# Spreading 1/rms rows by PE transposes, small column loads on the SP queue, and shared-expert parts dealt over 28 experts

## The chip, the cores and the metric

The kernel runs on one core of one Trainium2 chip. Its time is the device time of one launch in microseconds (us), the median of several runs. The profile is one execution recorded by the hardware profiler; its stages are given as us from the start of its span.

## The reference

Four sequences of 512 tokens with 512 features pass through a cross-attention layer and a mixture-of-experts layer. Cut to what matters:

```python
x = x + xattn(layernorm(x), ctx)        # ctx: 4 x 1601 x 512, the first 257 rows are image rows
x = x + ffn(layernorm(x))

# xattn: 16 heads of 32
q = rms_norm(x @ q_w.T + q_b, norm_q_w)             # norm over all 512 features
k = rms_norm(ctx_txt @ k_w.T + k_b, norm_k_w); v = ctx_txt @ v_w.T + v_b
k_img, v_img = ...                                  # the same with the image weights
out = (attention(q, k, v) + attention(q, k_img, v_img)) @ o_w.T + o_b

# ffn: 32 experts of width 256, 4 chosen per token, at most 80 tokens per expert
Y = (silu(Xp @ W_gate) * (Xp @ W_up)) @ W_down      # Xp: the tokens of each expert
out = scatter_add(Y * weight)
shared = (silu(x @ sg.T) * (x @ su.T)) @ sd.T       # width 512, for all tokens
return out + shared
```

Everything is computed in float32; only the shifts of the softmax are split into bfloat16 parts.

## The kernel before, in words

The order of all instructions is written out by hand: each engine executes its instructions in the order in which the program issues them, and buffers are rings of named tiles, so an instruction waits for its operands, and for its output's buffer to be read out.

**Start.** SP and ACT each issue a part of the first loads. ACT issues the four pieces of the key weight `first_wk`, two of the four tiles of x, and then, by `column` (L153 to L156), eight small columns of biases and norm weights and `o_b` (L197). A bias column is read with a stride, 512 elements of 4 bytes (`"(c p) -> p c"`). SP issues the first context block, the other two x tiles, four pieces of `q_w` and then whole blocks and weights. On TensorE (PE) the projections of the first context block run with the input chunk k outermost, over four PSUM banks: k = 0, 1, 2, then k = 3 (L636 to L649). Between them stand the tasks of the four x tiles: `norm` (ACT, L273) makes the layer-normed `xl`, `turn` (L279, L280) transposes it on PE, four 128x128 blocks a tile, and ACT copies it to `xlT`. Before the change two tiles are turned behind k = 2 and two behind k = 3. After them the projections of q from `xlT` begin.

**Keys and queries, per sequence b.** `feature_chunk` (L228) projects a block of keys or queries, four chunks of 128 features. ACT squares each (L235), DVE applies bias and norm weight (L236), GpSimd (POOL) sums the squares (L238). `norms` (L247) sums over features by matmuls with a column of ones, and POOL makes the column `r` of 1/rms, one value per token. `normed` (L253 to L261) needs that column as a row spread over all 128 partitions: for each 128 tokens PE multiplies the column, broadcast to [128, 128] as the stationary operand, by the identity, and DVE multiplies the chunk by the result in PSUM (L261). There are five calls per sequence: q, three text blocks (512, 512, 320 tokens) and the image block (257). Between them DVE takes the maxima of the first scores (L310).

**Attention.** Scores, exponentials (L374), sums and weighted values, with the maxima (L336) of the next chunk alongside.

**Experts.** The shared expert is cut into units. For the token blocks n = 0 to 2 they run ahead of the routed experts. The twelve units of the last block, n = 3 (eight gate/up projections, four down projections), form the list `between`. The loop over the 32 routed experts does for expert e: `gate_up(e)`, the gather of the tokens of expert e + 7 (POOL), `turn(e + 2)`, `down(e - 1)`, the weight loads of expert e + 4 (SP), and then those units of `between` that are due (L1104). In `down`, ACT scales the result to `y` (L1030, four buffers) and POOL issues an indirect DMA that adds its 80 rows into `out` (L1031). Each of these scatters waits until the previous one has landed, since all write `out`. The last down unit of the shared expert copies its part to `ys`, and POOL issues one DMA that adds 1024 KB into `out` (L977); it stands in the same chain of writers.

Of the kernel before, what the change touches and what calls it, by code (L numbers as in the profile page):

```python
# [18 lines left out]
P = 128  # L19
# [10 lines left out]
E, I, TOPK, NG, TKG = 32, 256, 4, 8, 3  # L30
# [28 lines left out]
@with_exitstack  # L59
def xattn_moe_kernel(ctx: ExitStack, tc: tile.TileContext, a: dict, out: bass.AP):  # L60
    nc = tc.nc

    dram = ctx.enter_context(tc.tile_pool(name="dram", bufs=1, space=DRAM))
    x1_d = dram.tile([T, D], F32, name="x1_d")

    xw_d = dram.tile([T, D + E], F32, name="xw_d")
    xnT_d = dram.tile([P, NC, T], F32, name="xnT_d")
    den_d = dram.tile([B * NC, 2 * NG4, L], F32, name="den_d")
    rec_d = dram.tile([B * NC, 2 * NG4, L], F32, name="rec_d")

    const = ctx.enter_context(tc.tile_pool(name="const", bufs=1))
    ident = const.tile([P, P], F32, name="ident")
    make_identity(nc, ident)
    mhalf = const.tile([P, 8], F32, name="mhalf")
    nc.gpsimd.memset(mhalf, -0.5)
    logits = const.tile([P, NT, E], F32, name="logits")

    with tc.manual_schedule():
        body(tc, a, ident, mhalf, logits, x1_d, xw_d, xnT_d, den_d, rec_d, out)
# [30 lines left out]
def body(ctx, tc, a, ident, mhalf, logits, x1_d, xw_d, xnT_d, den_d, rec_d, out):  # L110

    nc = tc.nc
# [12 lines left out]
    def psum(dt=F32):  # L125

        shape = [P, 512] if dt is F32 else [P, NQ, P]
        banks.append(banks.pop(0))
        return ring.tile(shape, dt, name="ps", tag=f"bank{banks[-1]}")
# [17 lines left out]
    def rowt(name):  # L147
        return row.tile([P, D], F32, name=name, tag="row")
# [3 lines left out]

    def column(name, src=None):  # L153
        t = w.tile([P, NC], F32, name=name, tag=name)
        nc.scalar.dma_start(t, a[name] if src is None else src)
        return t  # L156

    def bias_column(name):
        return column(name, a[name].rearrange("(c p) -> p c", p=P))
# [6 lines left out]
    def load_x(b, qt, queue=nc.sync):  # L166
        xt = rowt("xt")
        queue.dma_start(xt, a["x"][b, qt * P:(qt + 1) * P, :])
        return xt
# [13 lines left out]
    for k in range(NC):  # L183
        nc.scalar.dma_start(first_wk[:, k, :], a["k_w"][:, k, :])
        nc.sync.dma_start(first_block[:, k, :], a["ctxT"][0, k * P:(k + 1) * P, s0:s0 + n])
        if k in (1, 2):
            first_x += [load_x(0, len(first_x), nc.scalar), load_x(0, len(first_x) + 1)]
    for k in range(NC):
        nc.sync.dma_start(wq[:, k, :], a["q_w"][:, k, :])
    k_b, nk_w = bias_column("k_b"), column("norm_k_w")  # L190
    q_b, nq_w = bias_column("q_b"), column("norm_q_w")
    second_block = load_block(0, 1)
    wv = weight("v_w")
    ki_b, nki_w = bias_column("k_img_b"), column("norm_k_img_w")
    v_b, vi_b = bias_column("v_b"), bias_column("v_img_b")
    o_b = w.tile([P, D], F32, name="o_b")
    nc.scalar.dma_start(o_b, a["o_b"].partition_broadcast(P))  # L197
    rw = w.tile([P, NC, E], F32, name="rw")
    ones = w.tile([P, P], F32, name="ones")
    nc.gpsimd.memset(ones, 1.0)  # L200
# [26 lines left out]
    def feature_chunk(dst, xT, n, wt, bias, weights, c, ps, sq, k, at=0):  # L227


        to = slice(at, at + n)  # L230
        nc.tensor.matmul(ps[:, :n], lhsT=wt[:, k, c * P:(c + 1) * P], rhs=xT[:, k, to], start=k == 0, stop=k == NC - 1)  # L231
        if k < NC - 1:
            return
        s = rowt("sq")[:, :n] if c else sq[:, to]
        nc.scalar.activation(s, ps[:, :n], AF.Square, bias=bias[:, c:c + 1])  # L235
        nc.vector.tensor_scalar(dst[:, c, to], ps[:, :n], bias[:, c:c + 1], weights[:, c:c + 1], ALU.add, ALU.mult)  # L236
        if c:
            nc.gpsimd.tensor_tensor(sq[:, to], sq[:, to], s, ALU.add)  # L238
        elif n % P:
            nc.gpsimd.memset(sq[:, n:n + P - n % P], 1.0)  # L240
# [12 lines left out]
    def normed(dst, r, n):  # L253

        ps = psum()
        for s in range(-(-n // P)):
            m = min(P, n - s * P)
            nc.tensor.matmul(
                ps[:, s * P:s * P + m], lhsT=r[:, s:s + 1].to_broadcast([P, P]), rhs=ident[:, :m], start=True, stop=True
            )  # L260
        nc.vector.tensor_tensor(dst, dst, ps[:, :n].unsqueeze(1).to_broadcast([P, NC, n]), ALU.mult)  # L261

    def turned_x(xlT, qt, xt):
# [218 lines left out]
    def queries(b, xs, n):  # L482

        qT = kv.tile([P, NC, L], F32, name="qT", bufs=2)
        xlT = kv.tile([P, NC, L], F32, name="xlT", tag="xlT")
        sq = held("sq_q")
        turn = [turned_x(xlT, qt, lambda qt=qt: xs[qt]) for qt in range(NQ)]

        def part(c, at):
            ps = psum()  # L490
            for k in range(NC):
                feature_chunk(qT, xlT, n, wq, q_b, nq_w, c, ps, sq, k, at)

        return qT, sq, turn, [partial(part, c, at) for c in range(NC) for at in range(0, L, n)]
# [135 lines left out]
    qT, sq_q, turn, work = queries(0, first_x, L)  # L630
# [4 lines left out]
    for k in range(NC):  # L635
        if k == NC - 1:  # L636
            first_sq = rowt("sq_k")
            nc.vector.tensor_scalar(nq_w, nq_w, SM_SCALE, None, ALU.mult)
        for c, ps in enumerate(first_banks):
            feature_chunk(first_kT[:, :, :n], first_block, n, first_wk, k_b, nk_w, c, ps, first_sq if k == NC - 1 else None, k)  # L640
        if k == 0:
            turn[0][1]()
            turn[1][1]()
        if k == 2:
            for qt in (0, 1):
                turn[qt][2]()
                turn[qt + 2][1]()
    for qt in (2, 3):
        turn[qt][2]()  # L649
    ident_b = w.tile([P, P], BF16, name="ident_b")  # L650
    nc.vector.tensor_copy(ident_b, ident)

# [21 lines left out]
    for n in range(2):  # L674
        t = w.tile([P, NQ, P], BF16, name=f"parts{n}", tag=f"parts{n}")
# [6 lines left out]
    for b in range(B):  # L682
# [51 lines left out]
        def take_normed(x):  # L734
            k0 = 0 if x == "q" else BLOCKS[x][0]
            normed(qT if x == "q" else kT[:, :, k0:k0 + size(x)], rs[x], size(x))
# [60 lines left out]
        for c in range(NC):  # L797
# [7 lines left out]
            fill, done = [], 0  # L805
# [22 lines left out]
            for t in range(NKT):  # L828
# [8 lines left out]
                if t == 1:  # L837
                    if more:
# [3 lines left out]
                        done = 1  # L842
# [30 lines left out]
                if prepares:  # L873
                    if t == 0:
                        xs = []
                        qT_next, sq_next, turn, work = queries(b + 1, xs, P)
# [28 lines left out]
    def expert_weights(e):  # L905
        ws = []
        for name, shape in (("W_gate", [P, NC, I]), ("W_up", [P, NC, I]), ("W_down", [P, NI, D])):
            t = wgp.tile(shape, F32, name=name, tag=name)
            nc.sync.dma_start(t, a[name][e])
            ws.append(t)  # L910
        return ws
# [143 lines left out]
    weights, gather, turn, gate_up, down = expert_parts()  # L1055
# [36 lines left out]
    n_between, done = len(between), 0  # L1092
    for e in range(E + 1):
        if e < E:
            gate_up(e)
            if e + AHEAD < E:
                gather(e + AHEAD)
        if e + 2 < E:
            turn(e + 2)
        if e:  # L1100
            down(e - 1)
            if e + WEIGHTS - 1 < E:
                weights[e + WEIGHTS - 1] = expert_weights(e + WEIGHTS - 1)
        while done < n_between and done * (E - 15) < n_between * (e + 1):  # L1104
            between.pop(0)()
            done += 1

# [36 lines left out]
```

## Time and profile before

| | us |
|---|---|
| median of three runs | 1740.51 (1738.91 to 1740.76) |
| the profiled execution, its own time | 1738.34 |
| its span, first to last instruction | 1736.6 |
| PE busy | 1688.6 (97%) |
| DVE busy | 982.7 (57%) |
| POOL busy | 865.2 (50%) |
| ACT busy | 649.4 (37%) |
| first routed expert's activation (L1020) | starts at 1491.5 |
| last scatter (L1031) | starts at 1729.06 |

A busy PE is not PE at its peak, since the ends of matmuls are modelled. The page's rows give engine, line, output and inputs, shapes, count, busy us and mean ns of one; a row of the timeline begins with the start and the length in us, and ends, in brackets, with the engine's idle time before it and what ended that.

### The profile page before, as it was taken

To read this page: it belongs to the slowest core of one execution; us is meant where nothing else is said; L and a number is where in the kernel's file an instruction comes from. 1 tells how busy PE (TensorE), PEld (TensorE's weight loads), DVE (VectorE), ACT (ScalarE), POOL (GpSimd) and SP (SyncE) were. 2 spreads that over 40 slices of the span, in tenths; PEclk is the share of its full clock that TensorE was granted. 3 is DMA by queue.
4 is the path that set the end of the run, shared out by engine and by line. 5 is a ranking of instruction groups with operands and counts; after the bars stand their busy time and mean duration, and the time that the engine had idled before them with its cause. 6 is when DMAs were issued, how large, how long until landed. Compare 5 with 4: busy or idle time off the path is not lost. (4 is left out here: it accounts for less than half of the span.)

```text
span 1736.6 us, 29529 instructions
## 1 busy us (share of the span) xinstructions
PE 1688.6 (97%) x11825; PEld 890.4 (51%) x11825; DVE 982.7 (57%) x2016; ACT 649.4 (37%) x1378; POOL 865.2 (50%) x615
## 2 busy tenths in 40 slices
PE   8999999999999999999999999999999999999993
PEld 3564444456544444564444445644442454666772
DVE  4765554857555557967666579666557665111110
ACT  2135456611355565115555641255547110111110
POOL 3237977332668853327679523296792210323232
PEclk9999999999999999999999999999999999999997
DMA  7000000312000004020001040300012563587882
GB/s 229 1 2 1 27 27 2 114 63 69 30 2 26 27 15 150 21 79 13 27 2 27 14 162 8 110 8 14 2 38 87 172 218 95 183 258 245 281 282 34
DMA packets 68344, 137.34 MB, mean 79 GB/s; under 512 B 16112, under 2 KB 28528, under 8 KB 66160
## 3 DMA queue, kind: packets, MB, share of 16 engines
q1 hardware_dynamic: 58336, 121.73, 20.6%
q0 software_dynamic: 5648, 11.87, 3.4%
q10 hardware_dynamic: 4224, 1.87, 0.4%
q8 instruction: 93, 1.52, 0.4%
q14 instruction: 43, 0.35, 0.1%
HBM read 112.63 MB, written 22.81 MB: 78 GB/s over the span
## 5 line engine op out<-in xcount | busy, mean ns | idle before, releaser
L374 ACT ACTIVATE pT<-ps 128x512 f32<-128x512 f32 (+1 forms) x832 | 429.7, 603 | 342.2 <-PE ps L373 331.8
L336 DVE TENSOR_REDUCE mx<-ps 128x1 f32<-128x512 f32 (+1 forms) x576 | 330.8, 616 | 264.7 <-PE ps L322 264.7
L389 POOL TENSOR_TENSOR acc<-acc,pT 128x1024 f32<-128x1024 f32 x192 | 445.7, 2360 | 3.0 <-ACT pT L374 2.6
L381 PE MATMUL po<-pT,v 128*32 128x512 f32 (+2 forms) x1792 | 222.0, 603 | 0.0
L292 PEld LDWEIGHTS ps<-v_w,cT 128*128 128x128 f32 (+1 forms) x1408 | 168.9, 186 | 102.2 <-DVE mx L336 56.1
L373 PE MATMUL ps<-qT,kT 32*128 32x512 f32 (+1 forms) x1664 | 213.7, 587 | 0.0
L322 PE MATMUL ps<-kT,qT 32*128 32x512 f32 (+1 forms) x1536 | 206.1, 549 | 0.0
L292 PE MATMUL ps<-v_w,cT 128*128 128x128 f32 (+1 forms) x1408 | 197.7, 284 | 0.0
L231 PE MATMUL ps<-cT,wk 128*128 128x512 f32 (+1 forms) x384 | 155.2, 549 | 6.1 <-DMA wk<-in_k_w 6.1
L310 DVE TENSOR_REDUCE mx<-ps 128x1 f32<-128x512 f32 (+2 forms) x256 | 128.2, 563 | 5.6 <-PE ps L307 5.6
L1031 POOL DMA_INDIRECT out<-y,tok x32 | 45.4, 1418 | 160.3 <-ACT y L1030 91.3
L1021 DVE TENSOR_TENSOR ehT<-ehT,ps 128x160 f32<-128x160 f32 x32 | 10.3, 322 | 177.2 <-ACT ehT L1020 162.8
L231 PEld LDWEIGHTS ps<-cT,wk 128*128 128x128 f32 x384 | 70.3, 192 | 75.9 <-issue 54.9
L370 PEld LDWEIGHTS <-pick 32*128 32x128 bf16 (+1 forms) x832 | 21.6, 91 | 165.8 <-issue 164.1
L300 ACT COPY v<-ps 128x128 f32<-128x128 f32 (+1 forms) x208 | 59.7, 287 | 118.4 <-PE ps L292 117.9
L238 POOL TENSOR_TENSOR sq_k<-sq_k,sq 128x512 f32<-128x512 f32 (+2 forms) x48 | 49.7, 1035 | 104.9 <-ACT sq L235 104.6
L396 POOL TENSOR_TENSOR acc<-pT 128x1024 f32<-128x1024 f32 x24 | 56.1, 2362 | 87.0 <-ACT pT L374 54.4
L389 POOL TENSOR_TENSOR pT<-pT 65x1024 f32<-65x1024 f32 x24 | 56.0, 2354 | 86.6 <-PE po L381 77.8
L389 DVE TENSOR_TENSOR acc<-acc,pT 128x1024 f32<-128x1024 f32 (+1 forms) x72 | 97.7, 1404 | 2.1 <-ACT pT L374 2.1
L322 PEld LDWEIGHTS ps<-kT,qT 32*128 32x128 f32 x1536 | 82.0, 183 | 30.8 <-issue 10.1
L381 PEld LDWEIGHTS po<-pT,v 128*32 128x32 f32 (+2 forms) x1792 | 34.7, 107 | 118.6 <-issue 109.3
L370 PE MATMUL ps<-mT,pick 32*128 32x512 bf16 (+1 forms) x832 | 82.5, 385 | 2.5 <-ACT mT L361 2.5
(209 smaller groups left out, 2207.3 us busy)
## 6 DMA issues: line engine op xcount, KB each, us to landing
W_gate<-in_W_gate SPq DMA_DIRECT2D x32, 512.0 KB
W_up<-in_W_up SPq DMA_DIRECT2D x32, 512.0 KB
W_down<-in_W_down SPq DMA_DIRECT2D x32, 512.0 KB
rb<-rec_d SPq DMA_DIRECT2D x64, 128.0 KB
xt<-in_x SPq DMA_DIRECT2D x30, 256.0 KB
cT<-in_ctxT SPq DMA_DIRECT2D x7, 1024.0 KB
wki<-in_k_img_w SPq DMA_DIRECT2D x4, 1024.0 KB
wo<-in_o_w SPq DMA_DIRECT2D x4, 1024.0 KB
```

What stands on the lines that cost most here:

```text
L231: nc.tensor.matmul(ps[:, :n], lhsT=wt[:, k, c * P:(c + 1) * P], rhs=xT[:, k, to], start=k == 0, stop=k == NC - 1)
L292: nc.tensor.matmul(ps[lo:hi, :], lhsT=cTs[bl][:, k, at:at + hi - lo], rhs=ws[bl == NB - 1][:, k, c * P:(c + 1) * P], start=k == 0, stop=k ...
L300: nc.scalar.copy(v[:n, t, :], ps[:n])
L310: nc.vector.tensor_reduce(mx[:, qt, g, bl:bl + 1], ps[:, :n], AX.X, ALU.max, negate=True)
L322: nc.tensor.matmul(ps[:, j * n:(j + 1) * n], lhsT=qT[r:r + HD, c, q * P:(q + 1) * P], rhs=kT[r:r + HD, c, k0:k0 + n], start=True, stop=True,)
L336: nc.vector.tensor_reduce(mx[:, qt, g, i:i + 1], ps[:, :m], AX.X, ALU.max, negate=True)
L370: nc.tensor.matmul(ps[:n], lhsT=pick[r:r + HD, kind(t), :n], rhs=mT[r:r + HD, :], start=True, stop=False)
L373: nc.tensor.matmul(ps[:n], lhsT=kT[r:r + HD, c, t * P:t * P + n], rhs=qT[r:r + HD, c, :], start=False, stop=True)
L374: nc.scalar.activation(pT[:n, g, :], ps[:n], AF.Exp)
L381: nc.tensor.matmul(po[r:r + HD, :], lhsT=v[rows, t, r:r + HD], rhs=pT[rows, g, :], start=start, stop=stop)
L389: (nc.vector if idle else nc.gpsimd).tensor_tensor(to[rows, h, :], to[rows, h, :], pT[rows, h, :], ALU.add)
L396: (nc.vector if idle else nc.gpsimd).tensor_tensor(acc[:, h, :], pTs[0][:, h, :], pTs[1][:, h, :], ALU.add)
```

## The change

It has three parts. In `normed` the matmul with the identity becomes a PE transpose of the broadcast column; for a last part of m tokens only m rows are read. In the start, the small columns and `o_b` go to the SP queue, those of k ahead of `q_w`; and the turns stand one step earlier: two tiles behind k = 1 and two behind k = 2. In the loop over the experts the twelve units are dealt over 28 experts in place of 17: the last one comes behind expert 25 instead of 15.

```diff
     def column(name, src=None):
         t = w.tile([P, NC], F32, name=name, tag=name)
-        nc.scalar.dma_start(t, a[name] if src is None else src)
+        nc.sync.dma_start(t, a[name] if src is None else src)
...
+    k_b, nk_w = bias_column("k_b"), column("norm_k_w")
     for k in range(NC):
         nc.sync.dma_start(wq[:, k, :], a["q_w"][:, k, :])
-    k_b, nk_w = bias_column("k_b"), column("norm_k_w")
     q_b, nq_w = bias_column("q_b"), column("norm_q_w")
...
-    nc.scalar.dma_start(o_b, a["o_b"].partition_broadcast(P))
+    nc.sync.dma_start(o_b, a["o_b"].partition_broadcast(P))
...
             m = min(P, n - s * P)
-            nc.tensor.matmul(
-                ps[:, s * P:s * P + m], lhsT=r[:, s:s + 1].to_broadcast([P, P]), rhs=ident[:, :m], start=True, stop=True
-            )
+            nc.tensor.transpose(ps[:, s * P:s * P + m], r[:m, s:s + 1].to_broadcast([m, P]), ident[:m, :m])
...
-        if k == 2:
+        if k == 1:
             for qt in (0, 1):
                 turn[qt][2]()
                 turn[qt + 2][1]()
-    for qt in (2, 3):
-        turn[qt][2]()
+        if k == 2:
+            turn[2][2]()
+            turn[3][2]()
...
-        while done < n_between and done * (E - 15) < n_between * (e + 1):
+        while done < n_between and done * (E - 4) < n_between * (e + 1):
             between.pop(0)()
             done += 1
```

## The prediction

> **What bounds the kernel now.** I read the page first: PE is busy for 97% of the span, so up to the experts work taken from PE counts unless another engine is found beside it. The last of the 40 slices shows a 3, so the end is another matter; a table of three stretches of the expert loop shows it.
>
> ```profile
> PE 1688.6 (97%) x11825; PEld 890.4 (51%) x11825; DVE 982.7 (57%) x2016; ACT 649.4 (37%) x1378; POOL 865.2 (50%) x615
> PE   8999999999999999999999999999999999999993
> ...
> core 0: us, PE busy (x) PEld busy (x) DVE busy (x) ACT busy (x) POOL busy (x), PEclk, DMA share, GB/s
> 1486.00:1618.00 132.00, 131.70 (x766) 92.55 (x767) 14.94 (x38) 19.86 (x39) 37.16 (x32) 1.00 0.73 232
> 1618.00:1686.00 68.00, 66.61 (x481) 53.38 (x479) 7.93 (x22) 10.27 (x22) 18.99 (x16) 1.00 0.98 315
> 1686.00:1736.60 50.60, 20.16 (x124) 14.10 (x124) 2.81 (x8) 5.19 (x12) 14.92 (x11) 0.76 0.28 37
> ```
>
> In the last 50 us PE works for 20. What runs to the end is seen in POOL's timeline (L1031: scatter of one expert's rows; L977: the 1024 KB accumulate) and in the waits from 1630 on:
>
> ```profile
> 1612.16 1.42 POOL L1031 DMA_INDIRECT out<-y,tok  x1 [4.46 <-ACT y L1030]
> 1618.83 1.41 POOL L977 DMA_DIRECT2D out<-ys  x1 [5.25 <-ACT ehT L1020]
> 1633.71 1.48 POOL L1031 DMA_INDIRECT out<-y,tok  x1 [12.13 <-DMA out<-ys]
> ...
> 1724.35 1.39 POOL L1031 DMA_INDIRECT out<-y,tok  x1 [3.31 <-issue]
> 1729.06 1.39 POOL L1031 DMA_INDIRECT out<-y,tok  x1 [3.32 <-DMA out<-y,tok]
> ...
> ACT y L1030 <- DMA out<-y,tok: 52.1, 11, 7.2
> POOL out L1031 <- DMA out<-ys: 12.1, 1, 12.1
> ```
>
> The scatters are a chain: each waits for the landing of the one before. Scatter 14 (numbered by expert from 0) starts at 1612.16; the accumulate pushes scatter 15 to 1633.71, while ACT had its y at 1620.16. From then on PE, without shared units, would make an expert every 5.53 us (y at 1620.16 and 1625.69), and the chain needs (1686.17 - 1633.71) / 7 = 7.5 us. So y, with four buffers, waits 52 us for scatters, and the last scatters run alone, 4.7 us each. The end is set by the chain, not by PE.
>
> At the start PE stands still for ACT:
>
> ```profile
> 16.37 1.28 ACT L273 ACT_TABLE_LOAD   x1 [16.37 <-DMA k_img_b<-in_k_img_b]
> 18.53 0.66 PE L279 MATMUL ps<-ident,xl 128*128 128x128 f32 x4 [0.41 <-ACT xl L273]
> 19.43 0.66 PE L279 MATMUL ps<-ident,xl 128*128 128x128 f32 x4 [0.24 <-ACT xl L273]
> 26.00 3.70 PE L231 MATMUL ps<-xlT,q_w 128*128 128x512 f32 x8 [1.60 <-ACT xlT L280]
> ```
>
> **Part 1, the start.** Removed from ACT: nine DMA issues between 8.82 and 16.33 us. The statistics that `xl` needs are ready from 11.05 us (the POOL row of L216), so the table load (1.28) can lie ahead of that and the four `xl` (0.8 each) run from 11 us. On PE, k = 0 and 1 end near 14.7 (24 records end at 18.12, the last 8 take 3.4). Then 8 transposes (1.0, as at 23.36), k = 2 (3.5), 8 transposes (1.0) and k = 3 (3.5) give 23.7 for the first q matmul, against 26.00: the three idles, 0.41 + 0.24 + 1.60 = 2.25 us, go. ACT's copies of the last two tiles then lie under k = 3. Added to SP: nine issues, among them 640 small packets ahead of `q_w`. The four `q_w` issues end at 14.07 now, and DMA is busy for 82% from 14 to 18 us; the same packets cross the same engines on either queue. The two k columns were issued by ACT 1.3 us apart, so `q_w` moves by some 2.6 us at most, and has some 5 us before 23.7. Behind it on SP the q columns, the second block and v_w move back by as much again; the second block is first used at 41.6. `norm_q_w` is the one to watch: DVE waits for it (now until 14.90) ahead of its first L236 (22.36), and behind `q_w` it should land near 18. What is late next is the sum of squares on POOL (its third sum ends at 26.96 now, PE wants it at 29.11): both move together. The 2.25 us then cross a stretch that PE bounds. I take -2.3; bounds 0 (`q_w` late) and -2.5.
>
> **Part 2, the transposes.** Now: L258 has 144 matmuls, two records per product, in 20 calls. Eight weight loads take 0.89 us from the first to the next line's (383.94 to 384.83). The nearest row is the same operation on float32 tiles, L279: four, one record each, take 0.39 (592.54 to 592.93).
>
> ```profile
> 383.94 0.97 PEld L258 LDWEIGHTS ps<-ident,rrms 128*128 128x128 f32 x8 [0.76 <-issue]
> 384.83 0.30 PEld L231 LDWEIGHTS ps<-cT,wk 128*128 128x128 f32 x2
> ...
> 592.54 0.42 PEld L279 LDWEIGHTS ps<-ident,xl 128*128 128x128 f32 x4 [0.76 <-issue]
> 592.93 0.97 PEld L292 LDWEIGHTS ps<-v_w,cT 128*128 128x128 f32 x8
> ```
>
> So 0.5 us less for a call with four products, 0.4 with three: 12 x 0.5 + 8 x 0.4 = 9.2 us of PE. Not all is on the path. In the window 60 to 92 us DVE is busy for 30.65 of 32, in 376 to 406 for 28.52 of 30: there the maxima (L310) set the pace, and the calls of the second and third block fall into it, so nothing is taken for them. The calls of q and of the first block fall into 36 to 60 (DVE 9.48 of 24), and DVE stands idle 0.59 to 1.64 us ahead of the image block's L261, waiting for L258. That is 0.5 + 0.5 + 0.4 = 1.4 us for b = 0, 1, 2; for b = 3 DVE is full already at the first block (9.58 of 10 in 1040 to 1050), so 0.9. Sum 5.1, I take -5. A 64-row or one-row transpose has no row; from 80 rows (L1007, 4 in 0.44 us) I see no penalty.
>
> A rule speaks against this part. The Trainium skill, "TensorE: Matmul & The Clock Gate", Part 4: PE-mode transpose, gives about 275 ns for a 128x128 transpose inside a kernel and says that transposes don't hold the full clock. At 275 ns each, four cost 1.1 us, 0.2 more than now, and 20 calls would lose about 3 to 4 us. Here 273 ns is indeed the median duration of one L279 matmul, but they start 0.1 us apart, and the granted clock is 1.00 in 18 to 22 us with eight of them; the row decides. Ends: -9.2 (all on the path) and +4 (the rule).
>
> **Part 3, dealing the units.** PE's work is the same; its order changes. A unit takes 3.44 us (y at 1611.20 and 1620.16, 8.97 apart, less 5.53). Before, twelve units lie within experts 0 to 15. After, they come behind experts 0, 2, 4, 7, 9, 11, 14, 16, 18, 21, 23 and 25, so y comes every 5.53 + 12 x 3.44 / 28 = 7.0 us on average. y 24 would be ready at 1666.6 (first y at 1499.4, plus 24 x 5.53, plus ten units). The chain, under weight loads and gathers, took 7.1 to 8.0 us a step where it was seen to bind before 1612, 7.5 after. Steps of 6.5 and 6.7 occur too, so I take 7.3: scatter 24 starts at 1500.4 + 24 x 7.3 = 1675.6 (1667.6 if y bounds, 1680.4 at 7.5). Next in the chain stands the accumulate: +6.7 as at 1612.16 to 1618.83, so 1682.3. It held up the next scatter for 14.9 us when the DMA share was 1.03 to 1.10. Weight loads now end near 1686 and PE's pace puts their end at the same time after the change, so I take 11.5 for it, with ends of 9 and 14.9. Scatter 25 at 1693.8; six more at 4.65 without loads, 27.9: scatter 31 at 1721.7. Plus the 7.5 that follow the last scatter now: 1729.2 against 1736.6, so -7.4, rounded to -8 since part of the steps will be bound by y. The wait that takes the place of the backlog is the accumulate near the end. It is queued ahead of seven scatters on POOL, ACT's y 29 waits behind them, and PE's last down behind that. Ends: -17 (1667.6 + 6.7 + 9 + 27.9 + 7.5 = 1718.7, with a margin) and +1 (7.5 a step and 14.9: 1737.4).
>
> The same skill prices a DMA from GpSimd ("DMA: Bandwidth & Descriptors", Anatomy of one DMA) at about 2.0 us plus bytes over 436 GB/s: 4.4 us for 1 MiB. With that the part would bring -15. The row has 14.9 for it, an accumulate under load, so the rule is only my lower end.
>
> **Sum.** -2.3 - 5 - 8 = -15.3 us, against the profiled execution's 1738.34 (1736.6 of span and 1.7 around it), which is 2.2 below the median of the runs. I carry the difference to the median: 1740.5 - 15.3 = 1725.2, say 1725.
>
> **Rivals.** (a) The dealing brings nothing: steps of 7.5 us and the full 14.9 for the accumulate, part 3 at about 0. For it: the chain is as long as before, 32 scatters and one accumulate, and only the backlog at the end is rearranged. Against: before, the chain idles between experts 0 and 14, 112 us for 14 steps. Time 1733. Chance 0.12. (b) The slow side: the accumulate in the tail. If scatters beside the evenly spread weight loads take 8.0 us, near the worst seen (8.65, once), scatter 24 is at 1692.4, and 6.7 + 14.9 + 27.9 + 7.5 make 1749.4, +13; less 7.3 from the other parts, 1746. It decides from 7.9 us a step on, which four of the twelve loaded steps that bound reached singly; their mean is 7.5. Chance 0.05. (c) The start and the transposes don't do what they say (a late `q_w`, transposes at their full latency): 0 and +4, with -8 from part 3: 1736.5, near no change; chance 0.06, half of it faster by over the bound. My forecast has the rest, 0.77.
>
> **How the numbers follow.** About 0.2%, 3.5 us, is what a measurement of this kernel can tell from no change. The forecast and (a) are faster, (b) slower, (c) shared with "same": faster 0.92, same 0.03, slower 0.05. The range takes the forecast's lower ends without adding all of them (-2.5 - 7 - 16 = -25.5: 1715) and reaches up over (a) to 1736.
>
> **What would show it.** Right: first q matmul near 23.7 with no idle on `xlT`; 72 matmul records for L258's successor instead of 144, four in about 0.4 us; y 24 near 1660 to 1670 of the new span, the accumulate some 47 us before the end instead of 118, hardly any wait of y for scatters before it, six steps of about 4.65 behind it. Wrong: a wait of L231 on `q_w`, PE clock under 1.00 at the transposes, scatter steps of 8 us, or a span over 1733.

## The result and the profile after

The changed kernel takes 1721.37 us (median of four runs, 1721.01 to 1721.84) against 1739.95 us for the kernel before in runs on the same chip (1738.91 to 1740.76): a ratio of 0.9894, 95% interval 0.9877 to 0.9911, so about 1.1% less. The profiled execution took 1721.27 us (its span is 1719.6), 17.07 us less than the profiled execution of before; that one lies 1.6 us below its median, this one 0.1, so the traces show 17.1 us of the 18.6 between the medians. The line numbers after are a little smaller: L231 stays, L279 is now L277, L258 stays, L307 is L305, L1030 and L1031 are L1029 and L1030, and L977 is L976.

The page after: PE has 8.1 us less to do (1688.6 to 1680.5).

```profile
PE 1680.5 (98%) x11753; PEld 880.9 (51%) x11753; DVE 981.4 (57%) x2016; ACT 651.1 (38%) x1378; POOL 864.5 (50%) x615
```

The start, in PE's timeline after. No row behind the first carries a bracket, so PE stands still nowhere between its first matmul and the first of q, which begins at 23.51 instead of 26.00.

```profile
5.91 9.14 PE L231 MATMUL ps<-cT,wk 128*128 128x512 f32 x16 [5.91 <-DMA wk<-in_k_w]
14.89 1.04 PE L277 MATMUL ps<-ident,xl 128*128 128x128 f32 x8
15.76 3.60 PE L231 MATMUL ps<-cT,wk 128*128 128x512 f32 x8
19.20 1.04 PE L277 MATMUL ps<-ident,xl 128*128 128x128 f32 x8
20.07 3.60 PE L231 MATMUL ps<-cT,wk 128*128 128x512 f32 x8
23.51 3.60 PE L231 MATMUL ps<-xlT,q_w 128*128 128x512 f32 x8
```

The experts, in the table of stretches after. PE is busy throughout from 1600 to 1670 and then works for 27 of 50 us.

```profile
1600.00:1670.00 70.00, 70.00 (x444) 51.55 (x442) 7.22 (x20) 12.22 (x24) 21.59 (x18) 1.00 0.81 257
1670.00:1720.00 50.00, 26.98 (x180) 20.12 (x178) 2.81 (x8) 5.63 (x11) 9.90 (x7) 0.80 0.43 82
```

The end of the chain, in POOL's timeline after (L1030 is a scatter, L976 the accumulate), and under it a line of the waits of 1470 to 1720:

```profile
1654.73 1.42 POOL L1030 DMA_INDIRECT out<-y,tok  x1 [4.18 <-ACT y L1029]
1662.59 1.41 POOL L1030 DMA_INDIRECT out<-y,tok  x1 [6.44 <-DMA out<-y,tok]
1668.23 1.39 POOL L976 DMA_DIRECT2D out<-ys  x1 [4.22 <-DMA out<-y,tok]
1683.99 1.50 POOL L1030 DMA_INDIRECT out<-y,tok  x1 [14.37 <-DMA out<-ys]
...
1711.98 1.39 POOL L1030 DMA_INDIRECT out<-y,tok  x1 [3.31 <-DMA out<-y,tok]
```

```profile
ACT y L1029 <- DMA out<-y,tok: 1.3, 1, 1.3
```

ACT's wait for a free `y` has fallen from 52.1 us to 1.3: the backlog is gone. What stands at the end is still the chain. Scatter 24 starts at 1662.59, the accumulate at 1668.23, and it holds scatter 25 until 1683.99; the six that follow come 4.67 us apart, the last at 1711.98. Up to scatter 23 the row's releaser is often `y`: there PE still sets the pace. The last `y` is made at 1697.3, 14.7 us ahead of the last scatter.

Three marks split the 17.07 us, each a difference of two single executions: the first q matmul is 2.49 us earlier (start); the first scatter, 1500.38 before and 1493.20 after, is 7.18 earlier, so 4.69 more (transposes); the last scatter is 17.08 earlier, so 9.90 more (dealing).

### The profile page after: what moved, and what is told of

Read it like the earlier page. It is cut to its first block, busy times and chain, and to the rows that moved or that the text cites. A ratio compares the mean times of both kernels' runs of the same rounds, so it can differ in the third digit from the quotient of the medians.

```text
span 1719.6 us, 29395 instructions
## 1 busy us (share of the span) xinstructions
PE 1680.5 (98%) x11753; PEld 880.9 (51%) x11753; DVE 981.4 (57%) x2016; ACT 651.1 (38%) x1378; POOL 864.5 (50%) x615
## 5 line engine op out<-in xcount | busy, mean ns | idle before, releaser
L231 PE MATMUL ps<-cT,wk 128*128 128x512 f32 (+1 forms) x384 | 155.9, 551 | 5.9 <-DMA wk<-in_k_w 5.9
L1030 POOL DMA_INDIRECT out<-y,tok x32 | 45.5, 1423 | 151.6 <-DMA out<-y,tok 63.1
L231 PEld LDWEIGHTS ps<-cT,wk 128*128 128x128 f32 x384 | 70.3, 192 | 75.7 <-issue 55.1
```

## The experiments

"Alone" means that the edit is made to the kernel before. The twelve runs went to the chip in three groups, and each is compared with runs of the kernel before in its own group (medians 1739.1, 1739.62 and 1739.33 us).

### Each part alone

*The start alone.* Both halves of part 1, nothing else:

```diff
-        nc.scalar.dma_start(t, a[name] if src is None else src)
+        nc.sync.dma_start(t, a[name] if src is None else src)
...
-        if k == 2:
+        if k == 1:
             for qt in (0, 1):
...
-    for qt in (2, 3):
-        turn[qt][2]()
+        if k == 2:
+            turn[2][2]()
+            turn[3][2]()
```

> Part 1 alone on the kernel before. Theory: the three idles of PE ahead of the first q matmul go and stay gone, so it starts at 23.5 us instead of 26.0 and the time falls by 2.5 us. Rival (the saved time is used up before the experts, or the q weight is late): less than 1 us.

Measured: 1736.44 us, ratio 0.9985 (0.9978 to 0.9991), 2.7 us faster. The first q matmul starts at 23.34. In this trace the gain does not stay whole: the first scatter is 1.36 us early, since PE waits 1.72 us for DVE in the third sequence, and the last one 2.15.

*The transposes alone.*

```diff
-            nc.tensor.matmul(
-                ps[:, s * P:s * P + m], lhsT=r[:, s:s + 1].to_broadcast([P, P]), rhs=ident[:, :m], start=True, stop=True
-            )
+            nc.tensor.transpose(ps[:, s * P:s * P + m], r[:m, s:s + 1].to_broadcast([m, P]), ident[:m, :m])
```

> Part 2 alone on the kernel before. Theory of the prediction (calls beside a busy DVE bring nothing): -5 us. Rival A (every call counts, 0.4 to 0.5 us each): -8 to -9. Rival B (a transpose costs its full latency): +3 to +4. The shift of the first expert's activation shows it apart from the tail.

Measured: 1735.0 us, ratio 0.9973 (0.9962 to 0.9985), 4.1 us faster. In the trace the maxima of the last sequence are 4.24 us early, the first scatter 4.23 and the last scatter only 2.05.

*The dealing alone.*

```diff
-        while done < n_between and done * (E - 15) < n_between * (e + 1):
+        while done < n_between and done * (E - 4) < n_between * (e + 1):
```

> Part 3 alone on the kernel before. Theory (the chain of scatters is the bound from the first scatter on, and is independent of what came before): about -10 us, all of it after the first scatter, which starts at 1500.4 as before. Rival (the dealing gains only in company of the other parts): between -8 and -5.

Measured: 1729.46 us, ratio 0.9943 (0.9929 to 0.9956), 9.6 us faster. Its chain has the sizes of the changed kernel: 24 steps of 7.05 us, 5.48 to the accumulate, 15.65 behind it, six of 4.66. The size came as told, but not for the reason told: the chain is not the bound from the first scatter on, as the steps in the table further down show.

What follows: 2.7 + 4.1 + 9.6 = 16.4 us, against 18.6 for all together. The half-widths of the three intervals are about 1, 2 and 2.3 us, so the difference is not told from none: within that noise the parts add up.

### Which transposes count

The prediction took nothing for the calls of the second and third text block, because the maxima keep DVE busy there. This kernel leaves exactly those calls as they were:

```diff
-    def normed(dst, r, n):
+    def normed(dst, r, n, turned):
...
+            if turned:
+                nc.tensor.transpose(...)
+            else:
+                nc.tensor.matmul(...)
...
-            normed(qT if x == "q" else kT[:, :, k0:k0 + size(x)], rs[x], size(x))
+            normed(qT if x == "q" else kT[:, :, k0:k0 + size(x)], rs[x], size(x), x in ("q", 0, 3))
```

> Part 2 for three of the five calls of a sequence (q, first text block, image block), the second and third block as before. Theory of the prediction (the second and third call lie beside a busy DVE): the same time as with all five calls, within 1 us. Rival (PE's time counts there as well): only 3/5 of it, about 2 us slower than with all five.

Measured: 1737.78 us, ratio 0.9993 (0.9985 to 1.0002), 1.3 us faster, 2.8 less than with all five calls; the two intervals just touch. The two calls are worth something, as the marks below show too, and "nothing is taken for them" falls. How much, the medians don't say, for part of the loss has another cause. In its profiled execution PE waits 2.43 us for DVE in the last sequence, and the granted clock falls behind that wait (timeline, then the stretches of 3 us with PE, PEclk, DMA share and GB/s):

```profile
1050.74 1.14 PE L310 MATMUL ps<-kT,qT 32*128 32x512 f32 x8 [2.43 <-DVE kT L264]
```

```profile
1048.00:1051.00 3.00, 0.57 (x5) 1.00 0.00 0
1051.00:1054.00 3.00, 3.00 (x16) 0.71 0.00 0
1054.00:1057.00 3.00, 3.00 (x17) 0.72 0.08 13
```

At 0.71 and 0.72 the two stretches lose 3 x 0.29 + 3 x 0.28 = 1.7 us. Over the first two sequences, which have no such fall, the marks at the end of the maxima are 2.76 us early with all five calls and 1.62 with three: 1.14 us for four calls, 0.29 each, where PE saves 0.4 to 0.5 in one. (Where nothing ahead of the experts is changed, in the dealing alone, the same marks differ from those of before by 0.09.) The changed kernel agrees: in its first sequence the marks of `normed` move by 0.38 us for the second block and 0.45 for the third.

### The two halves of the start

*Only the columns go to SP* (the `-nc.scalar.dma_start` lines above; the turns stay behind k = 2 and k = 3):

> The columns on the SP queue alone, the turns where they were before. Theory (ACT's late start causes the first two idles, 0.65 us, and the place of the turns the third, 1.6 us): the first q matmul at about 25.2, -0.7 us. Rival (ACT's issues are the whole of it): -2.3.

Measured: 1739.64 us, ratio 1.0002 (0.9994 to 1.001): nothing.

*Only the turns stand earlier* (ACT keeps its nine DMA issues):

> The turns one step earlier alone, the columns on the ACT queue as before. Theory: the first layer-normed tile is ready at 18.5 us, as before, so PE, done with k = 1 at 14.9, now waits for it with k = 2 behind it: first q matmul at about 27.5, some 1 to 2 us slower than before. Rival (the place of the turns is the whole of it): -1.6.

Measured: 1742.58 us, ratio 1.0018 (1.0011 to 1.0025), 3.0 us slower. PE's timeline and stretches for the first, and then for the second:

```profile
25.82 5.40 PE L231 MATMUL ps<-xlT,q_w 128*128 128x512 f32 x8 [2.02 <-ACT xlT L280]
```

```profile
26.00:29.00 3.00, 3.00 (x6) 1.25 (x7) 2.65 (x12) 0.00 (x0) 0.77 (x1) 0.70 1.01 417
29.00:32.00 3.00, 3.00 (x13) 1.74 (x12) 2.21 (x19) 0.69 (x1) 0.00 (x0) 0.73 1.01 385
```

```profile
18.44 2.02 PE L279 MATMUL ps<-ident,xl 128*128 128x128 f32 x8 [2.94 <-ACT xl L273]
20.25 5.64 PE L231 MATMUL ps<-cT,wk 128*128 128x512 f32 x8
```

```profile
20.00:23.00 3.00, 3.00 (x7) 1.45 (x6) 0.00 (x0) 2.07 (x4) 0.00 (x0) 0.50 1.06 420
```

With the columns moved alone, `xl` is there early, but the last tiles are still turned behind k = 3, so PE waits 2.02 us for ACT's copy. With the turns moved alone, ACT is still issuing DMAs, and PE waits 2.94 us for `xl`. In both, what PE does next runs at a lower clock: eight matmuls take 5.40 or 5.64 us where 3.60 to 3.70 is usual. Both came out slower than expected; in these executions the matmuls at the lower clock lose 1.7 and 2.0 us. So neither half gains anything that could be measured without the other; ahead of the run each had been given a price of its own.

### What the accumulate costs in the chain

The changed kernel with the accumulate taken out of the chain of writers; SP stores the same 1 MB to a scratch tensor:

```diff
-                    to = out[n * L:(n + 1) * L, :].rearrange("(j p) d -> p j d", p=P)
-                    nc.gpsimd.dma_start(to, t["ys"], accum_op=ALU.add)
+                    to = x1_d[n * L:(n + 1) * L, :].rearrange("(j p) d -> p j d", p=P)
+                    nc.sync.dma_start(to, t["ys"])
```

> The changed kernel with the last shared block stored by SP to a scratch buffer instead of added into the output: the shared expert of the last 512 tokens is left out of the output, all else is computed, and the same 1024 KB are moved. Theory (the accumulate stands in the chain of scatters, 21 us for it and the landing ahead of it, and PE's own end comes next): scatter 25 follows 24 by 5 to 7 us, and the last scatter is set by the last y, some 13 us earlier: time about 1708. Rival (the scatters alone set the end): within 3 us of the changed kernel.

Measured: 1711.6 us (1711.53 to 1712.26), ratio 0.9841 (0.9826 to 0.9856), 9.8 us below the changed kernel and 3.6 above the 1708 told. Its POOL timeline:

```profile
1662.84 1.41 POOL L1030 DMA_INDIRECT out<-y,tok  x1 [6.06 <-DMA out<-y,tok]
1669.85 1.39 POOL L1030 DMA_INDIRECT out<-y,tok  x1 [5.59 <-ACT y L1029]
1678.90 1.39 POOL L1030 DMA_INDIRECT out<-y,tok  x1 [7.66 <-ACT ehT L1019]
...
1702.32 1.39 POOL L1030 DMA_INDIRECT out<-y,tok  x1 [3.32 <-DMA out<-y,tok]
```

The chain still sets the end without it, and not the last `y` as the theory had it: behind scatter 26 the steps are 4.68 us again, and the last scatter starts 3.9 us after its `y`. The accumulate costs 9.8 us of the end, not the whole 15.8 that scatter 25 waits. From scatter 24 to scatter 26 it takes 26.0 us with it and 16.1 without: scatter 25 then waits for its `y`, 7.0 us behind scatter 24, and scatter 26 comes 9.05 later, beside the weight loads and the store.

### Where it is cheap

Four kernels move the accumulate along the chain, or take away what runs beside it. Three of them differ from the changed kernel in one line, where `N` is 22, 32 or 34 for the 28 of the change (`E` is 32):

```diff
-        while done < n_between and done * (E - 4) < n_between * (e + 1):
+        while done < n_between and done * N < n_between * (e + 1):
```

> The changed kernel with the twelve units dealt over all 32 experts. Theory (the chain is full from the first scatter on, so its length does not depend on where the accumulate stands in it): within 3 us of the changed kernel, 1720 to 1724, with the accumulate behind scatter 28. Rival (later is better, since y comes faster): faster by 2 us or more.

> The changed kernel with the twelve units dealt over 22 experts instead of 28. Theory (y then comes every 7.4 us for 20 experts, slower than the chain could go, and that time is lost; the accumulate also meets more weight loads): 2 to 5 us slower than the changed kernel's 1721.4, so 1723.5 to 1726.5. Rival (an earlier accumulate leaves a shorter tail): faster, 1718 to 1720.

> The changed kernel with the twelve units dealt over 34 experts, so that the accumulate stands between the scatters of experts 30 and 31. Theory (once no weight loads run beside it the accumulate costs the chain 10 us wherever it stands): the same as with 32 experts within 1 us, 1715 to 1717. Rival (y of the last experts is then late by the units dealt between them, and with the accumulate last no slack is left behind it): 2 to 4 us slower than with 32, 1718 to 1720.

The fourth keeps 28 and spares the weight loads of the last four experts:

```diff
-            if e + WEIGHTS - 1 < E:
+            if e + WEIGHTS - 1 >= 28:
+                weights[e + WEIGHTS - 1] = weights[e - 1]
+            elif e + WEIGHTS - 1 < E:
                 weights[e + WEIGHTS - 1] = expert_weights(e + WEIGHTS - 1)
```

> The changed kernel without the weight loads of experts 28 to 31, which use the tiles of experts 23 to 26 instead; all else issues as before. Theory (the accumulate took 15.8 us from its start to the next scatter because weight loads ran beside it; with 32 experts it took 10.0 where none did): 10 to 11 us here, and the kernel 5 to 6 us faster than the changed one, 1715.5 to 1716.5, or a little more if the scatters beside it land sooner too. Rival (the price belongs to the place, behind scatters that are still under way, and not to the loads): 15 to 16 us, and the time within 1 us of 1721.4.

Measured, with the terms of the chain read from POOL's timelines (the first scatter is at 1493.2 to 1494.6 in all five):

| | time, us | ratio (95%) | steps before the accumulate | to the accumulate | from it to the next scatter |
|---|---|---|---|---|---|
| 22 experts | 1727.11 | 0.993 (0.9913 to 0.9946) | 19 of 7.45 | 5.64 | 16.09 |
| 28, the change | 1721.37 | 0.9894 (0.9877 to 0.9911) | 24 of 7.06 | 5.64 | 15.76 |
| 32 experts | 1715.99 | 0.9863 (0.9848 to 0.9879) | 28 of 6.76 | 4.58 | 9.97 |
| 34 experts | 1717.19 | 0.9875 (0.9858 to 0.9891) | 30 of 6.66 | 4.50 | 9.75 |
| 28, late weights spared | 1713.28 | 0.9849 (0.9833 to 0.9866) | 24 of 6.96 | 4.57 | 9.95 |

POOL's timeline with 32 experts, and then with 28 and the late weights spared:

```profile
1687.90 1.39 POOL L976 DMA_DIRECT2D out<-ys  x1 [3.19 <-DMA out<-y,tok]
1697.87 1.50 POOL L1030 DMA_INDIRECT out<-y,tok  x1 [8.59 <-DMA out<-ys]
```

```profile
1666.26 1.39 POOL L976 DMA_DIRECT2D out<-ys  x1 [3.16 <-DMA out<-y,tok]
1676.21 1.50 POOL L1030 DMA_INDIRECT out<-y,tok  x1 [8.56 <-ACT y L1029]
```

The last row names ACT's `y`, but that `y` was written by 1670.37; what the scatter waited for is the accumulate. And 10 us of the time in which it lands, in the tables of stretches of the changed kernel and of the one with 32 experts (PE to POOL busy, PEclk, DMA share, GB/s):

```profile
1670.00:1680.00 10.00, 10.00 (x73) 7.84 (x72) 1.44 (x4) 1.97 (x4) 0.00 (x0) 1.00 1.05 264
```

```profile
1690.00:1700.00 10.00, 7.92 (x43) 4.86 (x41) 0.32 (x1) 2.35 (x4) 1.50 (x1) 1.00 0.70 104
```

The steps before the accumulate follow `y` and not the chain. An expert without units takes PE 5.53 us and a unit 3.44, so `y` should come every 5.53 + 12 x 3.44 / N us: 7.41, 7.00, 6.82 and 6.74 by this estimate for 22, 28, 32 and 34, where 7.45, 7.06, 6.76 and 6.66 were measured.

The same 1 MB takes 10 us from issue to the next scatter where nothing runs beside it, and 16 where weights are loaded. With the late weights spared it takes 9.95 at almost the same place in the chain (1666.26 against 1668.23): it is the loads, not the place, and the rival of that run falls. That kernel is 8.1 us faster than the changed one, where 5 to 6 or a little more was told; its chain from the first to the last scatter is 209.8 us instead of 218.8, of which 5.8 is the accumulate, 1.1 the landing ahead of it and 2.3 a single step, from scatter 23 to 24 (5.53 instead of 7.86; up to scatter 23 both chains take 161.53 us). So the loads cost that scatter too.

With 32 the accumulate meets no loads, and the kernel is 5.4 us faster than the changed one: the theory that the chain is full from the first scatter on, and that the position of the accumulate therefore doesn't matter, fell. It is the best full version found. 34 is within 1.2 us of it, and the intervals overlap; 22 is 5.7 us slower than the change, a little more than expected. Moving the accumulate later brought nothing more once the loads had ended.

### In four pieces

Dealt over 34, and each down unit of the shared expert adds its own 256 KB:

```diff
-                if j == NQ - 1:
-                    to = out[n * L:(n + 1) * L, :].rearrange("(j p) d -> p j d", p=P)
-                    nc.gpsimd.dma_start(to, t["ys"], accum_op=ALU.add)
+                nc.gpsimd.dma_start(out[rows, :], t["ys"][:, j, :], accum_op=ALU.add)
```

> The changed kernel dealt over 34 experts, and the one accumulate of 1 MB split into four of 256 KB, each issued behind its own unit. Theory (each piece costs what its transfer and its landing cost, about 4.5 us, and all lie in the chain, since the chain has no slack): 4 times 4.5 is 18 for 10, so about 8 us slower than with one accumulate, 1723 to 1725. Rival (three of the four fall where POOL waits for y anyway, which comes every 6.8 us while the chain can go at 4.65 once the loads are over, so that only the last counts): about 5 us faster, 1710 to 1712.

Measured: 1723.8 us (1722.28 to 1727.68), ratio 0.9917 (0.99 to 0.9933), 6.6 us slower than in one piece. The end of its POOL timeline:

```profile
1708.82 0.92 POOL L974 DMA_DIRECT2D out<-ys  x1 [3.00 <-DMA out<-y,tok]
1713.85 1.47 POOL L1028 DMA_INDIRECT out<-y,tok  x1 [4.11 <-DMA out<-ys]
```

From a piece to the next scatter it is 5.43, 4.72, 4.80 and 5.03 us, 20.0 together against 9.75 for the whole: a link of this chain that carries 160 or 256 KB costs some 4.7 to 5 us where no loads run beside it, so four pieces cost about twice the whole. The theory holds in kind; the rival, that three pieces hide in POOL's waits, doesn't.

## Why the prediction was right, and where its steps were off

-15.3 us was told and -18.6 measured. The three parts are of the size forecast; inside parts 2 and 3 errors of both signs cancelled in part, and that is luck.

**The bound.** That the chain of writers sets the end is shown: taking one link out of it moves the end by 9.8 us with PE's work unchanged. That PE sets the time up to the experts is shown by the medians, 2.7 and 4.1 us lower with part 1 or part 2 alone. Single executions show it less well: 1.36 and 4.23 us at the first scatter became 2.15 and 2.05 at the last, for the chain itself took from 227.8 to 230.9 us in the six traces with the dealing of before.

**Part 1: -2.3 predicted, -2.49 in the trace, -2.7 alone.** The working held up to the first q matmul: 23.7 was told for it, 23.51 came, and the table load now lies at 8.88 instead of 16.37. `norm_q_w`, the column to watch, is used by DVE at 17.02, well ahead of 22. The lower end, `q_w` late, did not happen. The working did not ask what its two halves are worth without each other (nothing, and a loss). And "a stretch that PE bounds" is not true at the first block of the third sequence: there 1.6 us of the gain went into a wait for DVE in the trace of the start alone.

**Part 2: -5 predicted, -4.69 in the trace, -4.1 alone; the places were wrong.** What a call saves is as taken from the float32 transposes: the next line follows 0.44 us after the first of four matmuls (timeline after, around the first text block of the second sequence), where eight took 0.89.

```profile
365.94 0.60 PE L258 MATMUL ps<-ident,rrms 128*128 128x128 f32 x4
366.38 3.17 PE L231 MATMUL ps<-cT,wk 128*128 128x512 f32 x7
```

The clock stayed at 1.00 from 10 to 26 us, around the start's sixteen transposes, and from 365 to 367, so the rule that prices them at 275 ns each is not what this kernel pays. But the four sequences, for which 1.4, 1.4, 1.4 and 0.9 us were taken, gave 1.66, 1.91, -0.07 and 1.21 by the marks at the end of each sequence's maxima (`mT`, L361 before, L359 after). (With the transposes alone they gave 1.41, 1.35, 0.24 and 1.24.) Two steps failed and nearly cancelled. "Nothing is taken for them" was too little for the second and third block, some 0.29 to 0.45 a call. And the first block of the third sequence was taken to be on PE's path as in the first two; there PE now waits for DVE, as it does in the fourth, where nothing had been taken for that call. Timeline after, and then of before, where the third sequence has no such wait and the fourth a shorter one:

```profile
707.79 1.14 PE L305 MATMUL ps<-kT,qT 32*128 32x512 f32 x8 [2.01 <-DVE kT L259]
...
1045.86 1.14 PE L305 MATMUL ps<-kT,qT 32*128 32x512 f32 x8 [2.11 <-DVE kT L259]
```

```profile
1051.61 1.14 PE L307 MATMUL ps<-kT,qT 32*128 32x512 f32 x8 [0.95 <-DVE kT L261]
```

3.2 us more of waiting: PE arrives sooner, and DVE, which there works on the routing of the sequence before, doesn't. The prediction looked at DVE's load in the first, the second and the last sequence, not in the third. All nine kernels with the transposes wait 1.94 to 2.51 us there in the third sequence; the five without wait 0, 0, 0.68, 0.71 and 1.72. The spread among those five is one between executions: in the kernel with the dealing alone, where nothing changes ahead of the experts, the third sequence takes 0.72 us longer than in the profiled execution of before, and its wait is 0.68. The last section says where it comes from.

**Part 3: -7.4 worked out, -8 told, -9.9 in the trace, -9.6 alone.** The steps, against what was measured: 24 scatter steps at 7.3, measured 7.06 (-5.8 us in all); 6.7 to the accumulate, measured 5.64 (-1.1); 11.5 for the accumulate, measured 15.76 (+4.3); 27.9 for the last six, measured 28.0; 7.5 to the end, measured 7.6. Two terms are mis-sized. The accumulate was taken below the 14.9 of the trace because the loads were thought to end near 1686, a few us into it. It came earlier than told, and the loads ran beside it, at a DMA share of 1.05 from 1670 to 1680; that alone makes 16 of 10. The steps were taken too long, and this paid for it: they were priced as links of the chain, 7.3 us, where `y` set the pace. ACT's timeline after, the `y` of scatters 23 and 24:

```profile
1653.77 0.68 ACT L1029 ACTIVATE y<-ps,xp 80x512 f32<-80x512 f32 x1 [1.74 <-DMA xp<-xw_d,tok]
...
1659.30 0.68 ACT L1029 ACTIVATE y<-ps,xp 80x512 f32<-80x512 f32 x1 [1.74 <-PE ps L1025]
```

Scatter 23 (1654.73) starts 0.3 us after its `y` is written, as do nine others of the first 25, so the chain catches up with PE again and again; scatter 24 starts 2.6 us after its own. From the first `y` to `y` 24 it is 167.1 us, just what the prediction had worked out for it (24 x 5.53 and ten units), but had put aside as an end of its range. The price of 4.4 us from the page's formula is far off for an accumulate even without loads: 9.75 to 9.97 us from its issue to the next scatter.

**The rivals.** (a), that the dealing brings nothing, was right about the accumulate (more than the full 14.9) and wrong about the steps. (b) would have needed 7.9 us a step; they were 7.06. (c) fell with 23.51 and with four transposes in 0.44 us.

## What to carry to other kernels

When writes to one buffer form a chain, price its links before the engines: a link here costs 4.65 us with 160 KB and 4.7 to 5.0 with 256 KB where no loads run beside it, and about 10 with 1 MB, so fewer and larger ones win, and the largest belongs where no loads run beside it, not as early or as late as possible. Work out both paces, that of the producers and that of the chain: as long as the chain catches up, the producers set the time, and work spread over more of them shortens each step. And when PE is made faster in front of an engine that is nearly full, look up that engine's load at each place where the code runs, not at one: the gain turns into a wait there, and a wait of 2 us can cost the clock as well.

## What the hardware showed that was not expected

**A wait of 2 us can halve PE's clock, and its length doesn't decide.** PE kept 1.00 behind idles of 1.60 (before), 2.01 and 2.11 (after), 2.23 (22 experts) and 2.51 us (the four pieces), and lost it behind 2.02 (columns alone), 2.23 (late weights spared), 2.43 (three calls) and 2.94 us (turns alone). With the late weights spared, this is the clock behind the 2.23 us (stretches of 1 us; PE, PEclk, DMA share, GB/s):

```profile
708.00:709.00 1.00, 1.00 (x10) 0.86 0.00 0
709.00:710.00 1.00, 1.00 (x6) 0.50 0.05 16
...
712.00:713.00 1.00, 1.00 (x6) 0.94 0.00 0
```

It is at half for about 3.4 us and costs 1.7, and the third sequence of that execution takes 1.8 us longer than that of the changed kernel. The Trainium skill ("TensorE: Matmul & The Clock Gate", HAM oscillation — how this bites in real kernels) warns of idle gaps above some 3.4 us; here shorter ones sufficed, and the measurement decides. Its free-running window of that length (What's actually happening) could be why the same 2.23 us passes in one execution and not in another, but as the page has it a whole idle window is needed, and these idles are shorter; no run here shows the window, and the cause stays open.

**DVE beside POOL.** In the routing, 128x128 operations of one kind take 0.29 us, or up to 1.24 while POOL multiplies. DVE's and then POOL's timeline after, third sequence:

```profile
700.51 1.24 DVE L585 TENSOR_TENSOR space<-space 128x128 f32<-128x128 f32 x1
701.67 0.28 DVE L588 SCALAR_TENSOR_TENSOR space<-space 128x128 f32<-128x128 f32 x1
701.98 0.29 DVE L578 TENSOR_REDUCE space<-space 128x4 f32<-128x128 f32 x1
```

```profile
700.29 1.31 POOL L429 TENSOR_TENSOR po_s<-po_s,rb 128x512 f32<-128x512 f32 x1
701.67 1.40 POOL L430 TENSOR_TENSOR po_s<-po_s 128x512 f32<-128x512 f32 x1
```

The long ones here are TENSOR_TENSOR, and each ends within 0.15 us of the end of one of POOL's; the other two kinds stay at 0.28 and 0.29. SCALAR_TENSOR_TENSOR, which reads two tiles as well, is not spared everywhere: it took 1.35 to 1.38 us once each in the traces of the start, the columns and the dealing alone. The reductions, which read one tile, took 0.29 at most in the whole trace after. It fits the Trainium skill ("SBUF — State Buffer", Who interferes with whom), by which a DVE operation with two inputs from SBUF and a reading POOL exclude each other. This is what sets PE's wait at the first block of the third and fourth sequence. Add up, over DVE's 128x128 routing operations in the 12 us ahead of that block's L261 (L259 after), the time beyond 0.29 us each. In the third sequence the sum is 1.58 us in before and 1.81 with the turns alone, with no wait; 2.71, 2.75 and 3.76 with the dealing, the columns and the start alone, with waits of 0.68, 0.71 and 1.72; 3.10 in the changed kernel, with 2.01. Wherever PE waits, in either sequence, the wait is this sum less 2.04 without the transposes and less 1.10 with them, within 0.02 us in all fourteen traces. So where there is a wait, the 0.94 us that the transposes save PE ahead of that block goes into it, and the rest of it differs between executions with the time that DVE loses beside POOL.
